# The first half of head 1's projection ahead of head 0's sums, the second half behind them

## The chip, the cores and the metric

The kernel runs on one core of one Trainium2 chip. The metric is device time in microseconds (us), the median of several executions. A profiled execution gives a trace beside it: TensorE (PE, with its weight loads PEld), VectorE (DVE), ScalarE (ACT), GpSimd (POOL) and SyncE (SP), which mostly issues transfers. Each engine works through its own queue in order and waits there for what its next instruction needs.

## What is computed

Four graph layers on 512 nodes of 768 features and 8704 edges, each followed by a residual sum and a norm. The change lies in the first, a graph attention layer with eight heads and then a second one with one head:

```python
h = (x @ W).reshape(n, H, C)                       # H = 8 heads, C = 768
alpha_s = jnp.einsum('nhc,hc->nh', h, a_s)
alpha_d = jnp.einsum('nhc,hc->nh', h, a_d)
e = jax.nn.leaky_relu(alpha_s[src] + alpha_d[dst], NEG_SLOPE)
m = jax.ops.segment_max(e, dst, num_segments=n)
e = jnp.exp(e - m[dst])
denom = jax.ops.segment_sum(e, dst, num_segments=n)
alpha = e / (denom[dst] + EPS)
out = jax.ops.segment_sum(h[src] * alpha[:, :, None], dst, num_segments=n)
...
h = jax.nn.elu(gat_layer(x, W1, a_src1, a_dst1, b1, edge_index, concat=True))
out = gat_layer(h, W2, a_src2, a_dst2, b2, edge_index, concat=True)
```

## The kernel before

The edges are counted once into a dense 512 x 512 matrix, so that a softmax over neighbours becomes a row softmax over 512 columns, with the logarithm of the count added (`logs`), and the sum over edges a matrix product. Nodes lie in four blocks of 128 rows (`NB`), features in six chunks of 128 (`KC`).

For each head i of the first layer the kernel does this:

- **Projection** (`Head.project`, names g_p, g_h): x times the head's 768 x 768 weights, in two halves j of 384 columns. A half is a `product` of four blocks. To keep fp32 accuracy each operand is split into parts. A block is a `group`: twelve matmuls (L828 and L829), a scaling of the bank on ScalarE (L830), and six more matmuls (L835), which run after the next block's twelve; `close_group` runs the last block's. Then ScalarE copies the result (L1182), and in the second half two dot products on VectorE (L940) give the block's scores.
- **Softmax** (`Weights`): `keys` spreads the scores over a bank with four transposes (L948). `soft(b)` makes one block's weights: ScalarE L1152 and L932 (exp), VectorE L925, L927, L933, L934 and L936. `turn(b)` transposes them (four on TensorE, L1160, and one copy on ScalarE, L1163) into wT.
- **Sums** (`Head.aggregate`, g_o): for each of six chunks of columns four products (L1202) of h and wT; these need all four blocks of wT. Then comes the ELU, on ScalarE (L1209, L1212) and VectorE (L1213, L1215), and a split in three parts into the tile set Y (ScalarE L1219, VectorE L1220 and L1221). Its two helper tiles have two buffers each.
- **Second layer's product** (`Head.second`, g_s): Y times the head's rows of the second weights, again two halves of four blocks, added up in h2.

The weights come as a stream of units, a half of 384 columns each, in the order in which products use them. Units 0 and 1 are head 0's projection and are used whole (L881). Units 2 and 3 are head 1's projection, units 4 and 5 head 0's second product, and so on. `split_piece` loads a third of a unit into one of three raw buffers (SP, L770) and cuts it into parts w (ScalarE L785, VectorE L786 and L787). It is called after every block of a product, and it cuts only units up to the one after that in use. The parts have two buffers: unit 4 takes those of unit 2, unit 5 those of unit 3.

The code around the change runs in this order: head 0's projection with the counting between its blocks; head 1's projection, both halves, with head 0's `keys` after its first block and head 0's four `soft` after the four blocks of its second half; head 0's `turn` of all blocks; `turn_packed`, which transposes the packed counts (L1286), copies them on ScalarE into one of two buffers (L1289) and stores them (SP, L1290); the opening of Y's space, which lies where the counting tiles lay; and the loop over heads. In the loop head i's sums come first, then head i + 1's projection for i from 1 to 6 (for i = 0 it has been done), then head i's second product, between whose blocks head i + 1's softmax stands.

The code order is a priority and not a fixed sequence: a scheduler at compile time gives each engine its instructions, takes those of higher priority first where it holds them to be ready, and fills with later ones. `ahead` raises the priority of what is called in it.

Of the kernel before, what the change touches and what calls it, by code (L numbers as in the profile page):

```python
# [34 lines left out]
def gnn_stack_kernel(ctx: ExitStack, tc: tile.TileContext, a: dict, out: bass.AP):  # L35
# [28 lines left out]
    NB = N // P  # L64
# [4 lines left out]
    H0, H1 = a["L0_gnn_a_src1"].shape[0], a["L1_gnn_q1"].shape[1]  # L69
# [644 lines left out]
    def split_layers():  # L714
# [98 lines left out]
        def close_group():  # L813
            if open_group:
                open_group.pop()()
# [91 lines left out]
        def columns_of(j):  # L907
            return slice(j * HD, (j + 1) * HD)
# [30 lines left out]
        def dot(dst, h, row, junk):  # L939
            nc.vector.tensor_tensor_reduce(  # L940
                out=junk, in0=h, in1=row, scale=1.0, scalar=0.0,
                op0=ALU.mult, op1=ALU.add, accum_out=dst,
            )
# [57 lines left out]
        def ahead(f, *args):  # L1001

            with tc.high_priority(offset=AHEAD_BY):
                f(*args)


        with (
# [5 lines left out]
            def row_tile(name):  # L1013
                return hpool.tile([P, D], F32, tag="h", name=name)
# [14 lines left out]
            for name in ("edge_type_3", "edge_type_4", "dst", "src"):  # L1029
# [3 lines left out]
                f = pack.tile([NCH, P], F32, tag=f"{name}_r", name=f"{name}_f")  # L1033
# [10 lines left out]
            def edge_tile(name):  # L1044
                return pack.tile([P, NCH], F32, tag=name, name=name)
# [9 lines left out]
            for i in range(2):  # L1055
# [12 lines left out]
                f = edge_tile(f"fac{i}")  # L1068
# [98 lines left out]
            class Head:  # L1167
# [5 lines left out]
                    self.cols = small.tile([P, 2, NB], F32, tag="cols", name=f"{self.name}_cols")  # L1173
                    self.w = Weights(self.cols, self.name)

                def project(self, jobs=(), h=None):

                    self.h = h or [row_tile(f"{self.name}_h{b}") for b in range(NB)]
                    for j in range(2):

                        def keep(b, po, j=j):
                            nc.scalar.copy(self.h[b][:, columns_of(j)], po[:, :HD])  # L1182
                            if j:
                                for s in range(2):
                                    dot(
                                        self.cols[:, s, b : b + 1], self.h[b], self.rows[s],
                                        junk_row(f"{self.name}_j{b}_{s}"),
                                    )

                        now = jobs[NB * j : NB * (j + 1)]  # L1190
                        if whole:
                            product_whole(xT, whole.pop(0), keep, f"{self.name}_p{j}", now)
                        else:
                            product(S, keep, f"{self.name}_p{j}", now)
                    close_group()
# [85 lines left out]
            def turn_packed(b):  # L1281
# [3 lines left out]
                for i in range(NB):  # L1285
# [6 lines left out]
            head = Head(0)  # L1292
            jobs = [
                lambda: count(7),
                lambda: count(7),
                lambda: count(7),
                lambda: count(7),
                lambda: (count(7), split_x(0)),
                lambda: (count(NCH), split_x(1)),
                lambda: (ahead(decode, 0), split_x(2)),  # L1300
                lambda: (ahead(decode, 1), split_x(3)),
# [4 lines left out]
            after = Head(1)  # L1306
# [1 line left out]
                [  # L1308
                    head.w.keys,
                    lambda: None,  # L1310
                    lambda: None,
                    lambda: None,
                    lambda: ahead(head.w.soft, 0),
                    lambda: ahead(head.w.soft, 1),
                    lambda: ahead(head.w.soft, 2),
                    lambda: ahead(head.w.soft, 3),
                ],
            )
            for b in range(NB):
                ahead(head.w.turn, b)  # L1320
# [73 lines left out]
            for i in range(H0):  # L1394
                head.aggregate()
                jobs = []
                if 0 < i < H0 - 1:
                    after = Head(i + 1)
                    more = []
                    if i < 3:  # L1400
                        first = 2 * (i - 1)
                        more = [lambda: None] * 8
                        more[1] = lambda: decode3(first)
                        more[5] = lambda: decode3(first + 1)
                    elif i == 3:
                        more = [
                            lambda: None, check_counts, lambda: degrees(0), lambda: None,
                            lambda: None, lambda: degrees(1),
                        ]
                    elif i == 4:  # L1410
                        more = [lambda: None] * 8
                        more[2], more[5] = lambda: degrees(2), lambda: degrees(3)
                    after.project(more)
                if i + 1 < H0:
                    w = after.w
                    soft = [lambda b=b, w=w: w.soft(b) for b in range(NB)]
                    turn = [lambda b=b, w=w: w.turn(b) for b in range(NB)]
                    jobs = [
                        lambda: None, lambda: None, w.keys, lambda: (soft[0](), soft[1]()),
                        soft[2], lambda: (soft[3](), turn[0]()), lambda: turn[1](),  # L1420
                        lambda: (turn[2](), turn[3]()),
                    ]
                else:
                    cols = small.tile([P, 2, NB], F32, tag="cols", name="gl_cols")
                    w = Weights(cols, "gl")

                    def last_scores():
                        rows = work.tile([P, N], F32, tag="elu_e", name="gl_rows")[:2, :]
                        early.first_rows(Y)
                        early.last_rows(Y, rows)  # L1430
                        nc.vector.tensor_add(cols, parts, early.columns())

                    brow = row_on_all(work, a["L0_gnn_b2"], "gl_b", "arow")
                    xin = []
                    for b in range(NB):
                        xin.append(row_tile(f"xin0_{b}"))
                        nc.sync.dma_start(xin[b], a["x"][b * P : (b + 1) * P, :])

                    def bias(*blocks):
                        for b in blocks:  # L1440
                            nc.vector.tensor_add(xin[b], xin[b], brow)

                    soft = [lambda b=b: w.soft(b, divide=False) for b in range(NB)]
                    turn = [lambda b=b: w.turn(b) for b in range(NB)]
                    jobs = [
                        last_scores, w.keys, *soft, lambda: (turn[0](), bias(0, 1)),
                        lambda: (turn[1](), turn[2](), turn[3](), bias(2, 3)),
                    ]
                head.second(jobs)
                close_group()  # L1450
                if i + 1 < H0:
                    head = after
# [33 lines left out]
        with (  # L1486
# [113 lines left out]
            def project(left, r, j, name, also, jobs, copy):  # L1600
# [10 lines left out]
            jobs = [  # L1611
                lambda: None, lambda: (columns_of_rows(0), columns_of_rows(1)),
                lambda: (columns_of_rows(2), columns_of_rows(3)),
            ]
            first = [lambda: scores(0, 0)]
            for r in range(R3):
                for j in range(2):
# [4 lines left out]
                    if r == R3 - 1:  # L1622
                        blocks = [lambda: None] * NB
                    jobs = [
                        first.pop() if first else lambda: None,
                        lambda r=r, j=j, f=blocks: (scores(r, j), f[0](), f[1]()),
                        lambda r=r, j=j, f=blocks: (f[2](), f[3](), j and ((copy_scores(r), spread_keys(r), columns(r)))),
                    ]
# [425 lines left out]
        for i in (1, 2, 3):  # L2054
# [51 lines left out]
            for at, (r, j) in enumerate(order):  # L2106
                h = hs[r, j] = new_h(f"{name}_h{r}_{j}")
                jobs = ()
                if j == 0 and r < 2 or j == 1 and 1 <= r < R4 - 1:
                    to = r if j == 0 else r + 1  # L2110
                    fetch(to)
                    if i == 1:
                        jobs = [lambda: None] * 3 + [
                            lambda to=to: row_on_all_of(
                                rdeg_row[:, to, :], rdeg[:, to, :], f"rdeg{to}"
                            )
                        ]
                if i == 3 and at == 0:
                    jobs = [lambda b=b, brow=brow: add_bias(b, brow) for b in range(NB)]
                if i == 3 and (r, j) == order[-1]:  # L2120
                    jobs = [lambda: None, lambda: None, lambda: agg_rows(r, 0, 0), lambda: agg_rows(r, 0, 1)]
# [4 lines left out]
                if i == 1 and at == 1:  # L2126
                    jobs = first_jobs
                product(
                    S, lambda b, po, h=h: split_h(h, b, po), f"{name}_p{r}_{j}", jobs,
# [27 lines left out]
        for i in (1, 2):  # L2157
# [9 lines left out]
            for j in range(2):  # L2167
                h = hs[j] = new_h(f"{name}_h{j}")
                jobs = ()
                if i == 1 and j == 0:  # L2170
                    jobs = late_ends
                elif i == 1:
                    jobs = [lambda b=b: add_bias(b, brow) for b in range(NB)]
                elif i == 2 and j == 1:
                    jobs = [lambda: None, lambda: None, lambda: agg(0, 0), lambda: agg(0, 1)]
                product(
                    S, lambda b, po, h=h: split_h(h, b, po, dinv[:, b : b + 1]), f"{name}_p{j}", jobs
                )
            close_group()
            if i == 1:  # L2180
                for c in range(KC):
                    j, at = divmod(c, HK)
# [60 lines left out]
```

## Time and profile before

| | us |
|---|---|
| three runs, median (lowest to highest) | 1626.7 (1626.0 to 1627.7) |
| the profiled execution | 1624.3 |
| its span, first to last instruction | 1622.5 |
| TensorE busy / VectorE busy / ScalarE busy in it | 1584.8 / 1171.8 / 783.0 |
| granted TensorE clock, mean | 0.995 |

The stage of the change in windows of the same execution, each engine's busy time in us:

| window, us from the span's start | what TensorE does | PE | DVE | ACT |
|---|---|---|---|---|
| 70 to 79 | head 1's projection, first half | 9.00 | 8.06 | 7.59 |
| 79 to 87 | its second half | 8.00 | 8.00 | 4.97 |
| 87 to 95 | its end, transposes | 7.96 | 6.37 | 6.45 |
| 95 to 103 | head 0's sums | 8.00 | 7.22 | 2.91 |
| 103 to 115.4 | head 0's sums | 12.40 | 7.41 | 5.89 |
| 115.4 to 123.9 | head 0's second product, its start | 6.12 | 6.33 | 4.45 |
| 123.9 to 135 | head 0's second product | 11.10 | 6.15 | 8.60 |

Timeline lines in this document give the start in us, the length in us, the engine, the line of the kernel, the operation with the tiles it writes and reads, and how many were merged; in brackets stands the engine's idle time before it, and what ended it.

### The profile page before, as it was taken

What the parts mean: (1) busy time and instruction counts of PE and PEld (TensorE: products, weight loads), DVE (VectorE), ACT (ScalarE), POOL (GpSimd) and SP (SyncE); (2) the same over time, 40 slices, a digit from 0 to 9 for tenths busy, and PEclk for the clock granted to TensorE, in tenths of its full rate; (3) what the DMA queues carried; (4) which work ended last, traced back from release to release, by engine and by line L of the source; (5) the groups of instructions that cost most, each with busy time, mean ns of one, the idle gap of its engine ahead of it and who ended that gap; (6) DMA issues with size and microseconds to landing.
All of it is one profiled execution on the core that took longest, in us unless ns stands there. A gap on an engine that the chain in (4) does not pass through costs nothing.

```text
span 1622.5 us, 21155 instructions
## 1 busy us (share of the span) xinstructions
PE 1584.8 (98%) x8037; PEld 1356.6 (84%) x8037; DVE 1171.8 (72%) x2110; ACT 783.0 (48%) x1379; POOL 33.6 (2%) x64
## 2 busy tenths in 40 slices
PE   7999999999999999999999999999999999999997
PEld 4767979797878878866889976889989999999997
DVE  9976889888978697646785995556565568644784
ACT  7656566555555454334874481343344333333352
POOL 0000000000000000000001000000000000000000
PEclk9999999999999999999999999999999999999999
DMA  4241324232323122233104363322322234332211
GB/s 163 91 124 59 116 78 127 70 108 91 113 64 107 56 82 87 99 98 101 40 20 156 95 203 112 130 78 89 117 85 88 84 105 142 106 95 85 75 40 41
DMA packets 83790, 154.90 MB, mean 95 GB/s; under 512 B 6048, under 2 KB 67864, under 8 KB 82016
## 3 DMA queue, kind: packets, MB, share of 16 engines
q1 hardware_dynamic: 77920, 124.65, 24.8%
q0 software_dynamic: 4544, 25.60, 4.7%
q10 hardware_dynamic: 1216, 3.22, 0.5%
q8 instruction: 65, 1.06, 0.3%
q14 instruction: 45, 0.37, 0.1%
HBM read 138.22 MB, written 15.22 MB: 95 GB/s over the span
## 4 chain that ended last, share of the span: by engine, by line
PE 81%; DVE 11%; ACT 4%; issue 2%; DMA 2%; ACTq 0%; DVEq 0%; SPq 0%
PE g_o L1202 9%; PE c_p L835 6%; PE c_p L828 6%; PE c_p L829 6%; PE c_a L1987 5%; PE r_o L1900 4%; PE g_p L828 4%; PE g_p L829 4%; PE g_s L828 3%; PE g_s L829 3%; PE g_p L835 3%; PE g_s L835 3%; PE c_a L1975 2%; PE r_p L828 2%; PE r_p L829 2%; PE r_p L835 2%
## 5 line engine op out<-in xcount | busy, mean ns | idle before, releaser
L786 DVE SCALAR_TENSOR_TENSOR w<-w,raw 128x768 fp32r<-128x768 f32 x228 | 216.3, 953 | 116.1 <-ACT w L785 114.0
L785 ACT ACTIVATE w<-raw 128x768 fp32r<-128x768 f32 x228 | 190.0, 840 | 104.5 <-PE c_p L828 35.9
L787 DVE TENSOR_TENSOR w<-w,w 128x768 fp32r<-128x768 f32 x228 | 213.0, 950 | 10.4 <-PE c_root L835 4.4
L828 PE MATMUL c_p<-w,s 128*128 128x384 f32 x576 | 191.2, 335 | 0.0
L829 PE MATMUL c_p<-w,s 128*128 128x384 f32 x576 | 190.8, 334 | 0.0
L1202 PE MATMUL g_o<-wT,g_h 128*128 128x512 f32 x336 | 146.1, 594 | 1.2 <-ACT wT L1163 1.2
L1962 DVE TENSOR_TENSOR c_h_lo<-c_p,c_h_hi 128x384 fp32r<-128x384 f32 x96 | 53.1, 554 | 119.9 <-ACT c_h_hi L1961 119.8
L830 ACT ACTIVATE c_p<-c_p 128x384 f32<-128x384 f32 x96 | 45.3, 474 | 191.6 <-PE c_p L829 191.6
L828 PE MATMUL g_s<-w,y 128*128 128x384 f32 x384 | 132.4, 345 | 2.1 <-ACT y L1219 2.1
L1202 PEld LDWEIGHTS g_o<-wT,g_h 128*128 128x128 f32 x336 | 63.3, 190 | 80.2 <-issue 75.3
L829 PE MATMUL g_s<-w,y 128*128 128x384 f32 x384 | 129.1, 337 | 0.4 <-DVE y L1220 0.3
L835 PE MATMUL c_p<-w,s 128*128 128x384 f32 x576 | 117.2, 338 | 0.0
L828 PE MATMUL g_p<-w,s 128*128 128x384 f32 x336 | 115.2, 343 | 0.0
L829 PE MATMUL g_p<-w,s 128*128 128x384 f32 x336 | 112.4, 335 | 0.0
L829 PEld LDWEIGHTS c_p<-w,s 128*128 128x128 f32 x576 | 108.0, 188 | 0.8
L828 PEld LDWEIGHTS c_p<-w,s 128*128 128x128 f32 x576 | 107.9, 188 | 0.7
L835 PEld LDWEIGHTS c_p<-w,s 128*128 128x128 f32 x576 | 100.2, 188 | 4.3 <-ACT c_p L830 4.2
L835 PE MATMUL g_s<-w,y 128*128 128x384 f32 x384 | 78.5, 339 | 0.3 <-ACT g_s L830 0.3
L828 PEld LDWEIGHTS g_s<-w,y 128*128 128x128 f32 x384 | 72.3, 188 | 4.0 <-ACT y L1219 3.5
L1987 PE MATMUL c_a<-c_cT,c_h_lo 128*128 128x512 f32 x192 | 75.1, 391 | 0.0
L1987 PE MATMUL c_a<-c_cT,c_h_hi 128*128 128x512 f32 x192 | 75.1, 391 | 0.0
L829 PEld LDWEIGHTS g_s<-w,y 128*128 128x128 f32 x384 | 72.2, 188 | 2.1 <-DVE y L1220 1.5
(349 smaller groups left out, 3314.8 us busy)
## 6 DMA issues: line engine op xcount, KB each, us to landing
raw<-in_L_gnn_W_dram SPq DMA_DIRECT2D x216, 384.0 KB, 3.5
c_cT<-cT_store POOLq DMA_DIRECT2D x12, 1024.0 KB, 5.8
raw<-in_L_gnn_root_dram SPq DMA_DIRECT2D x18, 384.0 KB, 3.3
r_log<-log_store SPq DMA_DIRECT2D x8, 768.0 KB, 4.3
cT_store<-r_qk SPq DMA_DIRECT2D x20, 256.0 KB, 3.2
g_s<-in_L_gnn_a_src_dram POOLq DMA_DIRECT2D x8, 384.0 KB, 4.1
g_d<-in_L_gnn_a_dst_dram POOLq DMA_DIRECT2D x8, 384.0 KB, 4.5
log_store<-z SPq DMA_DIRECT2D x12, 256.0 KB, 3.2
```

The source lines that it names most:

```text
L785: nc.scalar.mul(hm, w, ROUND / SPLIT)
L786: nc.vector.scalar_tensor_tensor(lo, hm, -SPLIT, w, op0=ALU.mult, op1=ALU.add)
L787: nc.vector.tensor_sub(df, hm, lo)
L828: nc.tensor.matmul(out, l0, r0, start=(k == 0), stop=False)
L829: nc.tensor.matmul(out, l1, r1, start=False, stop=(k == KC - 1))
L830: nc.scalar.mul(out, out, SPLIT + 1.0)
L835: nc.tensor.matmul(out, l2, r2, start=False, stop=(k == KC - 1), skip_group_check=True)
L1202: nc.tensor.matmul(po, self.h[k][:, c * P : (c + 1) * P], wT[:, k, :], start=(k == 0), stop=(k == NB - 1),)
L1900: nc.tensor.matmul(po[:, :n], wT[:, k, :], source(k, at), start=(k == 0), stop=(k == NK - 1),)
L1962: nc.vector.tensor_sub(lo, po[:, :HD], hi)
L1975: nc.tensor.matmul(po[:, :HD], cT[:, k, bs], h[f][:, k, :], start=(k + f == 0), stop=(k == NB - 1 and f == 1),)
L1987: nc.tensor.matmul(po, h[f][:, k, cs], cT[:, k, :], start=(k + f == 0), stop=(k == NB - 1 and f == 1),)
```

## The change

`project` gets an argument that names the halves to do. Head 1's first half stays where the whole projection stood; head 0's four `soft` now come after its third and fourth block, two at a time, ahead of `turn` as before. The second half is done in the loop, behind head 0's sums and ahead of head 0's second product, with no other work between its blocks. The dot products of head 1 go with it, and so do its four calls of `split_piece`.

```diff
-                def project(self, jobs=(), h=None):
+                def project(self, jobs=(), h=None, halves=(0, 1)):
 
-                    self.h = h or [row_tile(f"{self.name}_h{b}") for b in range(NB)]
-                    for j in range(2):
+                    if 0 in halves:
+                        self.h = h or [row_tile(f"{self.name}_h{b}") for b in range(NB)]
+                    for j in halves:
...
                 [
                     head.w.keys,
                     lambda: None,
-                    lambda: None,
-                    lambda: None,
-                    lambda: ahead(head.w.soft, 0),
-                    lambda: ahead(head.w.soft, 1),
-                    lambda: ahead(head.w.soft, 2),
-                    lambda: ahead(head.w.soft, 3),
+                    lambda: (ahead(head.w.soft, 0), ahead(head.w.soft, 1)),
+                    lambda: (ahead(head.w.soft, 2), ahead(head.w.soft, 3)),
                 ],
+                halves=(0,),
             )
...
             for i in range(H0):
                 head.aggregate()
                 jobs = []
-                if 0 < i < H0 - 1:
+                if i == 0:
+                    after.project(halves=(1,))
+                elif i < H0 - 1:
                     after = Head(i + 1)
```

## The prediction

> **What bounds the kernel now.** First the busy shares on the profile's page. TensorE is busy for 98% of the span, so only a stretch in which it stands idle, or works with gaps, can give time back.
>
> ```profile
> span 1622.5 us, 21155 instructions
> PE 1584.8 (98%) x8037; PEld 1356.6 (84%) x8037; DVE 1171.8 (72%) x2110; ACT 783.0 (48%) x1379; POOL 33.6 (2%) x64
> ```
>
> Then TensorE's timeline around head 0's sums (start, length, line; in brackets the idle time before and what ended it), and the same place in heads 1 and 2.
>
> ```profile
> 65.58 0.63 PE L828 MATMUL g_p<-w,s 128*128 128x384 f32 x1
> ...
> 93.54 1.80 PE L1286 MATMUL pkt<-ident,packed_f 128*128 128x128 f32 x15
> 95.18 20.77 PE L1202 MATMUL g_o<-wT,h 128*128 128x512 f32 x48
> ...
> 118.94 0.44 PE L828 MATMUL g_s<-w,y 128*128 128x384 f32 x1 [1.59 <-ACT y L1219]
> ...
> 122.17 0.45 PE L828 MATMUL g_s<-w,y 128*128 128x384 f32 x1 [0.50 <-ACT y L1219]
> ...
> 123.91 1.32 PE L835 MATMUL g_s<-w,y 128*128 128x384 f32 x6
> ...
> 146.82 20.87 PE L1202 MATMUL g_o<-wT,g_h 128*128 128x512 f32 x48 [0.27 <-ACT wT L1163]
> ...
> 220.02 20.87 PE L1202 MATMUL g_o<-wT,g_h 128*128 128x512 f32 x48
> ```
>
> The sums of head 0 end at 115.4 us, and the second layer's product starts there at once on a Y that isn't finished. From 115.38 to the first L835 at 123.91 are 8.53 us, in which I count 28 matmuls. At the 0.1735 us from start to start of this kind they need 4.86 us, so 3.7 us are lost. After the sums of head 1 a projection follows instead, and its timeline has no such wait.
>
> Last, why Y is late, on ScalarE's timeline:
>
> ```profile
> 99.19 1.21 ACT L1289 CAST packedT<-pkt 128x512 int32<-128x512 f32 x2 [3.67 <-DMA packedT_store<-packedT]
> ...
> 105.32 0.63 ACT L1219 ACTIVATE y<-g_y 128x512 fp32r<-128x512 f32 x1 [3.66 <-DMA packedT_store<-packedT]
> ...
> 119.49 0.63 ACT L1212 ACTIVATE g_e<-g_e 128x512 f32<-128x512 f32 x1
> 121.49 0.63 ACT L1219 ACTIVATE y<-g_y 128x512 fp32r<-128x512 f32 x1 [1.37 <-DVE g_y L1215]
> ```
>
> Y lies where the counting tiles lay, so its first write waits for the last stores of packedT, until 105.32, which is 10.1 us into the sums. Six columns at 3.23 us each put the last high part at 121.49.
>
> **The change, part by part.** No arithmetic, transfer or weight cut is added; order alone changes.
>
> *The half that moves behind the sums.* It is 4 blocks of 18 matmuls at 3.12 us a block (the spacing of the L835 groups), 12.48 us of TensorE work that then lies where Y is being finished. I compare stages: from head 0's sums to head 1's are 146.82 - 95.18 = 51.64 us, without a projection. From head 1's to head 2's are 220.02 - 146.82 = 73.20 us, with a whole one and without the wait. With half a projection head 0 should take 73.20 - 12.48 = 60.72; at today's rate it would be 51.64 + 12.48 = 64.12. **Gain 3.4 us.** 12.48 us of cover is enough: Y's last part ends at 123.6, 8.2 us after the sums.
>
> *The half that no longer covers head 0's softmax.* Today 65.58 to 95.18 are 29.60 us; without 12.48 they are 17.12, so the sums could start at 82.70 if the softmax and its transposes were ready. TensorE ends the first half's four blocks at about 78.9 (the third L835 group starts at 76.78 and takes 1.04, the fourth follows). Then it has the 16 transposes of the weights (1.75 us) and the 16 of the packed counts (1.75 us), until 82.4. Is the softmax done? VectorE's timeline:
>
> ```profile
> 71.91 0.68 DVE L927 CUSTOM_DVE_ANT_0 z<-z,logs 128x512 f32<-128x512 f32 x1
> ...
> 80.40 0.68 DVE L927 CUSTOM_DVE_ANT_0 z<-z,logs 128x512 f32<-128x512 f32 x1
> 81.01 1.82 DVE L786 SCALAR_TENSOR_TENSOR w<-w,raw 128x768 fp32r<-128x768 f32 x2
> ...
> 84.61 0.47 DVE L936 TENSOR_SCALAR z<-z,g_den 128x512 f32<-128x512 f32 x1
> ```
>
> The fourth block ends at 85.08 today, but with weight cuts between its steps: after the second block's L927 at 71.91 to 72.5 the rest of the softmax is 2 x 1.28 (L925, L927) and 4 x 0.56 (L933, L934, L936) = 4.8 us of VectorE, and 0.9 us for the last exp. Its four jobs now stand in the first half, two to four blocks earlier than they did, ahead of the cuts of unit 4. Bounds: done at 72.5 + 4.8 + 0.9 = 78.2 with no cut between, 85.08 with today's. One cut (1.9 us) between gives 80.1, which I take since the cuts of unit 3 are still mixed in. The transposes (0.44), ScalarE's copy (0.5) and the hops end before 82. Cost 0 to 3.7 us, taken as 0.1, since the packed counts' transposes hide it. If the packed counts went first and the fourth block came at 85.08, the sums would start at 86.4: that is the 3.7.
>
> *ScalarE in its order.* Each product block needs one scaling on ScalarE (L830) before its L835. In head 1 that of the first block ran at 169.82, between the last L1212 (168.44) and the last L1219 (170.35). If head 0 gets the same order, it stands behind the last L1212, which ends 24.9 us after the sums' start (120.12 - 95.18) as long as Y's space comes 10.1 us into the sums. L830 is then done 25.5 after it; TensorE reaches the first L835 after the sums (20.2) and two blocks (24 x 0.1735 = 4.2), at 24.4. **Cost about 1 us**; 0 if the packed stores start earlier against the sums, as they may, since TensorE has nothing else to do behind the half. Queued behind L830 are the copies L1182 and the head's dots, due only for the keys some 20 us later. I take 0.6.
>
> *DMAs and queues.* Four cut calls move with the half, and with them three raw loads on SP, for units 4 and 5. Those could now stand on SP ahead of the packedT stores and wait there for a raw buffer, as today's eight loads from 68.46 to 94.5 do. Y then comes later; its end has room, 28.4 us into the sums (123.57) against 20.2 + 12.5 + 0.5 = 33.2 for the second product's start, 4.8 us, and only the L830 above feels it. POOL's rows for head 2 wait for head 1's dots, now about 17 us later, and head 2's projection is over 50 us away. Both costed at nothing: the cover is those 4.8 and 50 us.
>
> *Cuts of unit 4* (first weights of the second product) now stand in code behind the sums. Unit 5's stand behind them today, yet ran at 91.09 to 101 on ScalarE and VectorE, beside the sums' start, so code order doesn't hold them. Cost 0; the rival below prices the opposite.
>
> **Sum**: -3.4 + 0.1 + 0.6 = -2.7 us. The profiled execution took 1624.3 us (span 1622.5 and 1.8 around it); it becomes 1621.6. It lay 2.4 us under the median of 1626.7, so the median becomes **1624.0**.
>
> **Rivals.**
> 1. *The full gain*: ScalarE's order costs nothing, -3.3 to -3.9: 1623.2. For it: nothing but transposes competes with the packed stores. Against: Y has waited 3.7 us for them.
> 2. *The softmax becomes the wait*: the fourth block comes as late as today, the sums start at 86.4, +3.7; TensorE idles over 2 us and pays in clock. The row: in the second convolution 12 transposes took 2.44 us after 2.22 us idle, against 1.53 elsewhere, at a clock of 0.61:
>
> ```profile
> 834.51 2.44 PE L1685 MATMUL soft_wt<-ident,r_z 128*128 128x128 f32 x12 [2.22 <-ACT r_z L1669]
> 847.73 1.53 PE L1685 MATMUL soft_wt<-ident,r_z 128*128 128x128 f32 x12 [0.21 <-ACT r_z L1669]
> ```
>
> So -3.4 + 3.7 + 0.9 = +1.2; the sums start later against the stores, so ScalarE costs nothing: 1627.9. The Trainium skill ("TensorE: Matmul & The Clock Gate", What's actually happening) halves the clock only after an idle window of about 3.4 us; by that rule the 0.9 would fall away and the rival give 1627.0. The row has the drop after less, so the row decides. For this rival: 81.01 to 84.6 today. Against: TensorE could take product blocks of the moved half instead.
>
> 3. *Slower: unit 4's cuts come late.* If they are run after Y's chain, VectorE is free of Y 28.4 us after the sums' start (123.57 - 95.18), at 111.1, and has head 1's dots (8 x 0.96) and three cuts (3 x 1.9) before it: 13.4 us, to 124.5. The second product would start at 82.7 + 20.2 + 12.5 + 0.5 = 115.9 and get 2.8 us far on the first pieces: stall 5.8, and 0.9 for the clock. -2.7 + 6.7 = +4.0: 1630.7. It decides once the first cut of unit 4 starts after 111 us. Against it: unit 5's early cuts today, and cover that VectorE then has at 83 to 92.
> 4. *The order hardly changes*: TensorE is given the moved half before the sums all the same, because the weights aren't ready. Then little changes: 1626.5. Against: the transposes come first wherever they are ready.
>
> **How the numbers follow.** Forecast (-1.9 to -3.4) 0.34; full gain 0.30; softmax 0.16; late cuts 0.14; order unchanged 0.06. A measurement here tells about 0.2% (3.25 us) from no change. The full gain lies above it, and 0.07 of the forecast at its edge: faster 0.37. The rest of the forecast (0.27), the unchanged order (0.06) and 0.10 of the softmax case are within it: 0.43. Slower are the late cuts (0.14) and a softmax that ends later than today's (0.06): 0.20. The likeliest case alone spans 1623.3 to 1624.8; the range goes from the whole gain with 0.6 us more, 1622.4, to 1629.0, which leaves out part of the late cuts.
>
> **What would show it.** Right: no wait on y at L828 and L829 of head 0's second product; head 0's sums start at 82 to 83.5; 60.7 to 61.7 us from them to head 1's; L830 of the moved half's first block not over 1 us behind its L829. Wrong: idle on wT (L1163) before L1202, unit 4's L785 later than 95, a y wait in the second product, or a clock under 1.00 between 78 and 116.

## The result and the profile after

| | kernel before | changed kernel |
|---|---|---|
| median of 8 runs each (lowest to highest) | 1626.3 us (1623.9 to 1627.7) | 1621.0 us (1620.5 to 1622.6) |
| ratio, with its 95% interval | | 0.997 (0.9959 to 0.9981) |
| the profiled execution, its span | 1622.5 us | 1620.8 us |

By these runs the change makes the kernel 5.3 us faster, 3 to 7 by the interval. The two profiled executions differ by only 1.7 us. Both numbers have to be explained, and they aren't explained by the same thing.

First the page's head of the changed kernel: TensorE's work is the same, and the share of busy time hasn't moved.

```profile
span 1620.8 us, 21158 instructions
PE 1584.6 (98%) x8037; PEld 1356.6 (84%) x8037; DVE 1172.5 (72%) x2110; ACT 783.0 (48%) x1379; POOL 33.6 (2%) x64
```

TensorE's timeline at the stage of the change, in the changed kernel (start, length, engine and line; in brackets idle time before and what ended it):

```profile
65.78 0.63 PE L828 MATMUL g_p<-w,s 128*128 128x384 f32 x1
...
76.23 1.27 PE L1160 MATMUL g_wt<-ident,z 128*128 128x128 f32 x8 [0.58 <-DVE z L936]
...
79.66 1.12 PE L1160 MATMUL g_wt<-ident,z 128*128 128x128 f32 x8
80.53 1.83 PE L835 MATMUL g_p<-w,s 128*128 128x384 f32 x9
82.20 1.91 PE L1287 MATMUL pkt<-ident,packed_f 128*128 128x128 f32 x16
83.95 20.77 PE L1203 MATMUL g_o<-wT,h 128*128 128x512 f32 x48
...
108.72 1.20 PE L835 MATMUL g_p<-w,s 128*128 128x384 f32 x6
...
116.27 1.31 PE L835 MATMUL g_p<-w,s 128*128 128x384 f32 x6
...
121.40 1.20 PE L835 MATMUL g_s<-w,y 128*128 128x384 f32 x6
...
144.89 5.42 PE L1203 MATMUL g_o<-wT,g_h 128*128 128x512 f32 x12 [0.27 <-ACT wT L1163]
```

The waits on y before the second product are gone: the 24 matmuls ahead of the first L835 of g_s run without a gap, one of them ahead of the last L835 group of g_p and 23 behind it. From the first L828 to head 1's sums the stage takes 79.11 us, against 81.24 before. In front of the sums a short wait on z has appeared, and they start at 83.95 us, later than the 82 to 83.5 that was named as a sign.

ScalarE's timeline of the changed kernel shows that Y is nearly as late as it was, 9.0 us into the sums against 10.1, behind the same stores. It no longer matters:

```profile
86.78 1.20 ACT L1290 CAST packedT<-pkt 128x512 int32<-128x512 f32 x2 [1.83 <-DMA packedT_store<-packedT]
...
92.97 0.63 ACT L1220 ACTIVATE y<-g_y 128x512 fp32r<-128x512 f32 x1 [3.75 <-DMA packedT_store<-packedT]
...
107.70 0.47 ACT L830 ACTIVATE g_p<-g_p 128x384 f32<-128x384 f32 x1
109.16 0.63 ACT L1220 ACTIVATE y<-g_y 128x512 fp32r<-128x512 f32 x1 [0.99 <-DVE g_y L1216]
```

On TensorE, VectorE, ScalarE and GpSimd the order of instructions is the same in both profiles from 126 us on (124.5 us in the changed kernel), within head 0's second product, so what differs later is timing.

### The profile page after: what moved, and what is told of

Read it like the earlier page. It is cut to its first block, busy times and chain, and to the rows that moved or that the text cites. A ratio compares the mean times of both kernels' runs of the same rounds, so it can differ in the third digit from the quotient of the medians.

```text
span 1620.8 us, 21158 instructions
## 1 busy us (share of the span) xinstructions
PE 1584.6 (98%) x8037; PEld 1356.6 (84%) x8037; DVE 1172.5 (72%) x2110; ACT 783.0 (48%) x1379; POOL 33.6 (2%) x64
## 4 chain that ended last, share of the span: by engine, by line
PE 85%; DVE 9%; ACT 4%; issue 1%; DMA 1%; ACTq 0%; DVEq 0%
PE g_o L1203 10%; PE c_p L835 6%; PE c_p L828 6%; PE c_p L829 6%; PE c_a L1987 5%; PE g_s L828 4%; PE g_s L829 4%; PE r_o L1900 4%; PE g_s L835 4%; PE g_p L835 4%; PE g_p L828 3%; PE g_p L829 3%; PE c_a L1975 2%; PE r_p L828 2%; PE r_p L829 2%; PE r_p L835 2%
## 5 line engine op out<-in xcount | busy, mean ns | idle before, releaser
L828 PE MATMUL c_p<-w,s 128*128 128x384 f32 x576 | 191.2, 335 | 0.0
L830 ACT ACTIVATE c_p<-c_p 128x384 f32<-128x384 f32 x96 | 45.3, 474 | 191.6 <-PE c_p L829 191.6
L828 PE MATMUL g_s<-w,y 128*128 128x384 f32 x384 | 131.9, 343 | 0.0
L835 PE MATMUL c_p<-w,s 128*128 128x384 f32 x576 | 117.2, 338 | 0.0
L828 PE MATMUL g_p<-w,s 128*128 128x384 f32 x336 | 115.8, 345 | 0.0
L828 PEld LDWEIGHTS c_p<-w,s 128*128 128x128 f32 x576 | 108.0, 188 | 0.7
L835 PEld LDWEIGHTS c_p<-w,s 128*128 128x128 f32 x576 | 100.2, 188 | 4.3 <-ACT c_p L830 4.2
L835 PE MATMUL g_s<-w,y 128*128 128x384 f32 x384 | 78.4, 339 | 0.3 <-ACT g_s L830 0.3
L828 PEld LDWEIGHTS g_s<-w,y 128*128 128x128 f32 x384 | 72.3, 188 | 1.0 <-ACT y L1220 0.7
```

The lines of the kernel that those rows point to most:

```text
L828: nc.tensor.matmul(out, l0, r0, start=(k == 0), stop=False)
L830: nc.scalar.mul(out, out, SPLIT + 1.0)
L835: nc.tensor.matmul(out, l2, r2, start=False, stop=(k == KC - 1), skip_group_check=True)
```

## The experiments

### Both kernels again: how much lies in the stage?

No edit: the kernel before and the changed one, each as it is.

Kernel before:

> The kernel before once more. Theory A (the medians differ by more than the stage because executions of one and the same kernel differ elsewhere by 2 to 4 us): ratio 1.000, runs again spread over 1624 to 1628, and the profile shows head 0's stage as before (sums of head 0 to sums of head 1 51.6 us) while the stretch after head 1's sums differs from the first profile by 1 us or more somewhere. Theory B (the change gains outside its stage, in every execution): the two profiles of the kernel before agree within 0.3 us in every stage.

Changed kernel, first time:

> The changed kernel once more. Theory A: the stage from the first L828 of head 1's projection to head 1's sums takes 79.1 us again (81.2 before), and the total is 2 to 3 us under the kernel before, ratio 0.998 to 0.999. Theory B: ratio 0.997 again, with 3 us gained behind head 1's sums in the profile.

Changed kernel, second time:

> The changed kernel a third time, to settle how far its total lies under the kernel before. Theory A (stage -2.2 us, and what goes beyond it is the scatter of executions of both kernels): -2.0 to -3.5 us. Theory B (3 us more outside the stage): -5 us.

| | runs | median us | ratio (95%) |
|---|---|---|---|
| before again | 11, against 33 | 1624.9, against 1625.4 | 0.9995 (0.9986 to 1.0004) |
| changed, first time | 11, against 33 | 1622.4, against 1625.4 | 0.9979 (0.9970 to 0.9988) |
| changed, second time | 10, against 24 | 1622.1, against 1626.5 | 0.9977 (0.9967 to 0.9986) |

With these, the gain is 3.0 to 4.4 us. Over all timed runs up to here the means are 1625.7 (76 runs) and 1622.0 (29): 3.7 us. The 5.3 of the first eight was a favourable draw. The changed kernel's stage takes 79.11, 79.12 and 79.09 us in three profiles, so it hardly varies. Theory B (3 us more outside the stage) found nothing in the traces: behind head 1's sums the changed kernel's three executions take 1475.8 to 1476.5 us and the first two of the kernel before 1475.7 and 1476.2. Theory A was right about the scatter: from 785 to 834 us the second profile of the kernel before lies 1.6 us further behind the first than at head 1's sums, since in the second layer its clock was at 0.50 for 6.8 us instead of 3.4; then a fall in the first makes it even again. But A was short as well: by its stage of -2.2 us the medians should not have come out over 3 us apart.

### The softmax jobs alone

Both halves stay ahead of the sums; only head 0's softmax jobs are moved forward.

```diff
                 halves=(0,),
             )
+            after.project(halves=(1,))
...
-                if i == 0:
-                    after.project(halves=(1,))
-                elif i < H0 - 1:
+                if 0 < i < H0 - 1:
```

> Only the softmax jobs are moved as in the change; both halves of head 1's projection stay ahead of head 0's sums. Theory A (the gain is the cover of Y): the wait on y in head 0's second product is back, 3.7 us lost there, head 0's sums to head 1's 51.6 us, total as before within 0.7 us. Rival (the earlier softmax brings the gain): head 0's sums start 1 us or more earlier than 95.2 us and the total is 2 us under before.

Measured 1625.8 us, ratio 1.0004 (0.9995 to 1.0013): no gain, and the sums start at 96.46, later than before. The wait on y is back, TensorE's timeline:

```profile
119.13 0.44 PE L828 MATMUL g_s<-w,y 128*128 128x384 f32 x1 [0.86 <-ACT y L1220]
...
122.37 0.44 PE L828 MATMUL g_s<-w,y 128*128 128x384 f32 x1 [2.07 <-ACT y L1220]
```

So the gain is the cover and not the earlier softmax. From head 0's sums to head 1's this execution took 54.55 us, 2.9 more than the 51.64 of the first profile. Y's first write came 12.3 us into the sums instead of 10.1, and the granted clock was 0.50 from 124 to 126 us. The last experiment of this section follows that up.

### Y's space free earlier, no half moved

The kernel before, with the packed counts turned and stored ahead of head 1's projection.

```diff
+            for b in range(NB):
+                turn_packed(b)
             after = Head(1)
             after.project(
...
             for b in range(NB):
                 ahead(head.w.turn, b)
-            for b in range(NB):
-                turn_packed(b)
```

> The kernel before with the packed counts' transposes and stores put ahead of head 1's projection, so that Y's space comes free early; both halves ahead of the sums. If Y is late because of the stores: the first write of Y comes some 5 us after head 0's sums start instead of 10.1, and the wait in head 0's second product falls from 3.7 to about 1 us, total -2.7 us without any half moved. Rival (Y is late through its own chain of 3.2 us a column): the first write comes earlier but the second product waits 2 us or more.

Measured 1623.2 us, ratio 0.9985 (0.9976 to 0.9994): 2.2 us faster with no half moved. The stores were what made Y late. ScalarE's timeline has the first write of Y waiting for its data and no longer for a store, and TensorE's timeline has no wait on y:

```profile
104.69 0.63 ACT L1219 ACTIVATE y<-g_y 128x512 fp32r<-128x512 f32 x1 [2.27 <-DVE g_y L1215]
```

It came 8.3 us after the sums' start (96.40) and not the 5 expected. A last L835 group stands between the sums' first matmuls (96.85 to 98.3), which accounts for about 1 us of that; the rest isn't separated. Part of the gain is paid back earlier: one L835 of head 1's projection waits 1.41 us for its L830.

### The same on the changed kernel

The same edit as above, on the changed kernel.

> The changed kernel with the packed counts' transposes and stores ahead of head 1's projection as well. If the moved half already covers all of Y's lateness: no y wait before and none after, head 0's sums to head 1's stay at 60.9 us, total within 0.7 us of the changed kernel; the counts' transposes no longer fill TensorE while ScalarE copies the last of wT, so up to 1 us may be lost there. If lateness still cost something behind the sums: 1 us or more gained.

Measured 1625.2 us, ratio 0.9996 (0.9988 to 1.0005), 3 us slower than the changed kernel measured beside it. Y's first write came 6.3 us into the sums instead of 9.0, and the stage behind the sums is 60.93 us, unchanged, so lateness costs nothing there any more. The loss is ahead of them and larger than expected. ScalarE's timeline, then TensorE's:

```profile
71.73 0.59 ACT L1290 CAST packedT<-pkt 128x512 int32<-128x512 f32 x1 [0.83 <-DMA packedT_store<-packedT]
72.21 2.43 ACT L1152 ACTIVATE z<-g_k,g_cols 128x512 f32<-128x512 f32 x4
75.15 0.59 ACT L1290 CAST packedT<-pkt 128x512 int32<-128x512 f32 x1 [0.50 <-DMA packedT_store<-packedT]
75.76 1.28 ACT L932 ACT_TABLE_LOAD   x1
...
78.48 0.47 ACT L830 ACTIVATE g_p<-g_p 128x384 f32<-128x384 f32 x1
```

```profile
79.00 2.29 PE L835 MATMUL g_p<-w,s 128*128 128x384 f32 x6 [3.00 <-ACT g_p L830]
```

The casts wait for a store, and the softmax and a table load stand behind them, all ahead of the L830 that TensorE needs. TensorE idles for 3 us, and from 78.0 to 84.8 the clock is 0.50.

### No half ahead of the sums

```diff
-            after.project(
-                [
...
-                ],
-                halves=(0,),
-            )
+            head.w.keys()
+            for b in range(NB):
+                ahead(head.w.soft, b)
...
-                    after.project(halves=(1,))
+                    after.project()
```

> Both halves of head 1's projection behind head 0's sums, so nothing of it covers head 0's softmax unless the scheduler takes it ahead. If the first half is the softmax's needed cover: TensorE idles for wT, or the scheduler runs blocks of the projection there all the same; with idle, head 0's sums start 5 us or more later against the work done, total +3 us or more over the changed kernel. If cover doesn't matter: within 1 us of the changed kernel.

Measured 1632.0 us, ratio 1.004 (1.0028 to 1.0052), 9.9 us over the changed kernel. TensorE's timeline, and the window before it (busy PE, PEld, DVE, ACT, POOL, then the clock, the DMA share and GB/s):

```profile
75.97 3.91 PE L1160 MATMUL g_wt<-ident,z 128*128 128x128 f32 x16 [8.07 <-DVE z L936]
```

```profile
68.00:76.00 8.00, 0.03 (x1) 0.03 (x1) 8.00 (x26) 7.31 (x15) 0.90 (x2) 0.63 0.49 147
```

Some cover is needed. The scheduler took no block of the projection ahead to fill the gap. Why not, this run doesn't show.

### The transposes not raised

The changed kernel with `head.w.turn(b)` in place of `ahead(head.w.turn, b)`.

> The changed kernel, with head 0's transposes of the weights no longer raised in priority. If the 1.05 us that the sums start later than forecast come from transposes queued on TensorE before their weights were ready (0.58 us idle on z, and changes between kinds of matmuls): the idle on z goes, the sums start 0.6 to 1 us earlier, total -0.6 us against the changed kernel. If they come from ScalarE's order (L830 behind four L1152): nothing changes.

Measured 1621.5 us, ratio 0.9974 (0.9964 to 0.9984), against 0.9977 for the changed kernel measured beside it: not told apart. The wait on z is gone, but another has come, on ScalarE, for the half's last block:

```profile
79.30 1.32 PE L835 MATMUL g_p<-w,s 128*128 128x384 f32 x6 [0.67 <-ACT g_p L830]
```

First L828 to head 0's sums takes 17.97 us, against 18.17, so of the expected 0.6 us only 0.2 are there. The span of its profile, 1618.9 against 1620.8 to 1621.5, is lower by more than that, and most of it lies far behind the edit. The window from 1532 to 1540 us, between the third layer and the last, first of this kernel and then of the changed one, has the same TensorE work, but not the same clock:

```profile
1532.00:1540.00 8.00, 5.83 (x44) 5.55 (x43) 8.00 (x20) 4.74 (x12) 0.00 (x0) 1.00 0.00 0
```

```profile
1532.00:1540.00 8.00, 5.83 (x33) 5.48 (x32) 7.99 (x22) 3.93 (x10) 0.00 (x0) 0.79 0.00 0
```

From the transposes of rdeg (L948, at 1044 us) to the end this execution needed 574.81 us, and the changed kernel's three 576.34 to 576.67.

### Four more profiled executions of the kernel before

No edit. Does the clock fall at the gap that the change closes?

First (b_look1):

> The kernel before, one more profiled execution. Theory C (TensorE's gaps at head 0's second product make the granted clock fall to 0.5 there in some executions and not in others, which adds 1.5 to 3 us to some runs of before and to none of the changed kernel): an execution with 0.5 between 118 and 128 us takes 1626.5 us or more, and its stage from the first L828 to head 1's sums 83 us or more; one without it takes 1623 to 1625.5 and 81.2 to 81.4 us. Theory D (the scatter lies in the last stages only): the stage is 81.2 to 81.4 us in all.

Second (b_look2):

> As b_look1: by theory C at least one of the looks at before shows the clock at 0.5 between 118 and 128 us and a stage of 83 us or more; by theory D none does.

Third (b_look3):

> As b_look1 and b_look2: by theory C the stage takes 81.2 to 81.4 us with the clock at 1.00 there, or 83 us or more with 0.5; by theory D always the former.

Fourth (b_look4):

> As b_look1 to b_look3: by theory C the stage takes 81.2 to 81.4 us with the clock at 1.00 there, or 83 us or more with 0.5; by theory D always the former.

| kernel before | first L828 to head 1's sums, us | longest single wait on y, us | lowest clock, 118 to 128 us | time, us |
|---|---|---|---|---|
| first profile | 81.24 | 1.59 | 1.00 | 1624.3 |
| second profile (b_rep) | 81.40 | 1.77 | 1.00 | 1625.3 |
| b_look1 | 84.75 | 2.07 | 0.50 | 1627.6 |
| b_look2 | 81.47 | 1.87 | 1.00 | 1625.4 |
| b_look3 | 81.92 | 1.55 | 0.50 | 1624.3 |
| b_look4 | 82.44 | 2.06 | 0.50 | 1625.1 |
| mean | 82.20 | | | 1625.3 |

Windows of b_look1, columns as above:

```profile
118.00:120.00 2.00, 0.88 (x2) 0.37 (x2) 1.27 (x3) 1.84 (x3) 0.00 (x0) 1.00 0.00 0
120.00:122.00 2.00, 0.00 (x0) 0.00 (x0) 1.28 (x3) 0.65 (x2) 0.00 (x0) 0.70 0.00 0
122.00:124.00 2.00, 1.92 (x5) 1.52 (x6) 1.92 (x4) 1.19 (x2) 0.00 (x0) 0.50 0.00 0
124.00:126.00 2.00, 2.00 (x8) 2.00 (x7) 1.27 (x3) 0.63 (x1) 0.00 (x0) 0.50 0.00 0
126.00:128.00 2.00, 2.00 (x9) 2.00 (x8) 0.67 (x1) 0.10 (x1) 0.00 (x0) 0.59 0.00 0
```

The same stretch in b_look2:

```profile
118.00:120.00 2.00, 0.45 (x1) 0.19 (x1) 1.30 (x2) 1.32 (x3) 0.00 (x0) 1.00 0.00 0
120.00:122.00 2.00, 1.94 (x10) 1.69 (x10) 1.79 (x4) 0.63 (x2) 0.00 (x0) 1.00 0.00 0
```

Theory C holds in its core: the clock falls at this gap in three of six executions of the kernel before, and in none of the three profiles of the changed one, where no gap is left. Theory D is out. C's sizes were too large: b_look3 and b_look4 cost 0.5 to 1.2 us, not over 1.6, and came out at ordinary totals. There the clock was at 0.50 for 3.4 us, in b_look1 for 6.8. That is the bad case, and it has a second part: its stores were slower, so that Y's first write came at 108.41, 12.3 us into the sums instead of 10.1.

## Why the prediction was wrong

The time lies outside the range, 1621.0 against 1622.4 to 1629.0. The mechanism, the sign and the place were right. What failed were sizes: the first term of the sum, which was read from a single execution; the smaller term for ScalarE's order; and the base from which the sum was taken off. The softmax's term erred the other way.

- *The gain of the moved half, forecast 3.4 us.* This is the term that was mis-sized. Against the one execution it was read from, it came out at 3.2 (51.64 + 12.48 - 60.94). But that execution was the mildest of six. Over the six profiles of the kernel before, head 0's sums to head 1's takes 52.64 us on average and not 51.64, and 55.19 at worst, so that the half's cover is worth 52.64 + 12.48 - 60.94 = 4.2 us. The stall that was removed had two prices that the forecast left out: the stores vary, and the clock falls in some executions. The forecast had a row for the clock (2.44 us after 2.22 us idle, against 1.53) and charged it to the stalls that might come, not to the one that goes.
- *The clock's price in the rivals, 0.9 us.* That row was a sample too. In nine profiles of the two kernels the same twelve transposes always wait 2.22 us. In seven of them they ran at a full clock (1.53 us, 1.42 for the 11 recorded in one); the clock fell in the first profile of the kernel before and in the third of the changed one (2.44 and 2.05 us). After this idle time the 0.9 was the price in one execution, and not what the stall costs each time. The changed kernel's first profile has:

```profile
833.50 1.53 PE L1685 MATMUL soft_wt<-ident,r_z 128*128 128x128 f32 x12 [2.22 <-ACT r_z L1669]
```

- *The softmax without its cover, forecast 0.1 us of 0 to 3.7.* It cost 1.05 (18.17 against 17.12). The softmax itself was ready at 80.0, as forecast (80.1). Part of the cost are the transposes raised on TensorE before their weights were there, with 0.58 us idle. The run without the raise lost this wait but got 0.67 us idle on ScalarE instead and gained 0.2 us, so where the rest goes isn't shown.
- *ScalarE's order, forecast 0.6 us.* This term failed as well: it cost nothing that the trace shows. L830 did come between the last L1213 and the last L1220, but Y's space had come 1.1 us earlier against the sums (92.97 - 83.95 = 9.0 against 10.1), and it was done at 108.17, before TensorE asked at 108.72.
- *Unit 4's cuts, forecast 0.* Right: they ran from 79.13 to 84.95 on ScalarE, until 1 us past the sums' start, although they stand behind them in the code.
- *The base and the range.* The sum was taken off 1626.7, the median of three runs, but the 76 runs of the kernel before have a mean of 1625.7. Of the 3.0 us between 1624.0 and the measured 1621.0, 1.0 is this base, 1.0 the larger gain (3.7 against 2.7 over all runs), and 1.0 the luck of the first eight (1621.0 against the mean of 1622.0). Luck alone doesn't excuse the range, since 1622.0 lies below it too. The runs of the kernel before lie up to 5.7 us apart (1622.3 to 1628.0), those of the changed kernel 2.8 (1620.5 to 1623.4).
- *The sum as measured.* With these sizes it is -4.2 + 1.05 + 0 = -3.1 us, which is also the stage's difference on average, 82.20 - 79.11. The 3.7 of all runs is 0.6 more, and no trace shows where. In the profiles the changed kernel is 0.7 us slower behind head 1's sums (means of 1476.1 and 1475.4 us). Its three profiled executions, 1622.6 to 1623.3, were among its slower ones. The clock also falls in the second layer, in every profile but not equally often, and behind the third, once in each of these nine. Whether the change shifts how often isn't settled.

The rivals: the full gain (-3.3 to -3.9) was the nearest to the 3.7. The late softmax, the late cuts and the unchanged order didn't occur.

## What to carry to other kernels

A stall read from one execution is a sample. Where it hangs on a transfer, look at several executions before taking its length for its price, and charge the clock to a stall that is removed just as to one that is added. Take the base of a forecast from many runs too; the three used here lay 1.0 us above the mean of 76. Work that was ready on TensorE was worth more behind the sums, where TensorE waited for Y, than ahead of them; but enough of it has to stay at the earlier chain, since taking all of it away cost 8 us of idling there. Before moving work as cover, ask what makes the chain late: here taking the stores earlier got more than half of the gain with two lines moved, and both together lost it again.

## What the runs showed of the hardware

TensorE's clock halved after stretches with gaps in some executions and not in others, with the same work. The length of a single gap didn't decide it: at head 0's second product the clock fell after waits of at most 1.55 us (b_look3) and stayed at 1.00 with one of 1.87 (b_look2). At 834 us it fell after 2.22 us idle in two of nine profiles. Between the third layer and the last a gap of 2.17 us stands in all nine, and the clock fell in each; the run without the raised transposes has the same gap there, and it didn't fall (the window from 1532 to 1540 us at 0.79 and 1.00, both with 5.83 us of TensorE work).

The falls have one length: behind the third layer the clock was at 0.50 for 3.4 us in each of the nine, at head 0's second product for 3.4 us (120.7 to 124.1 in b_look3) or twice that (120.8 to 127.6 in b_look1).

The Trainium skill ("TensorE: Matmul & The Clock Gate", What's actually happening) describes a free-running window of about 3.4 us, which would make the outcome depend on where the gap falls in it, and has the clock at half after at least one idle window. The length of the falls and the chance that the runs show fit such a window, but the runs have falls after gaps far shorter than 3.4 us. No run here shows the window itself.
